# A pool for gathered expert rows, clears and square roots on ScalarE, and three shared parts behind the expert blocks, in an eight-stage adaLN network

## The chip, the cores and the metric

The kernel runs on one core of a Trainium2 chip, as one program and one launch. The metric is the device time of one execution in microseconds (us); the time of a kernel is the median of several executions. The core has a matrix engine (TensorE, PE in the profile), a vector engine (VectorE, DVE), an engine for activations (ScalarE, ACT), a general engine (GpSimd, POOL) and a queue processor (SyncE, SP). Each works through its own list of instructions in order; they wait for one another by semaphores. ScalarE looks functions such as Exp, Ln and Gelu up in a table that has to be loaded first, by an instruction of its own.

## The reference, cut to what matters

The network has four layers on 32 sequences of 256 tokens with 128 features. Each layer has two halves of the same form, with shift, scale and gate from a condition vector of each sequence:

```
for L in range(4):
    h = layernorm(x) * (1 + ca) + sa;  x = x + ga * attn_L(h)
    h = layernorm(x) * (1 + cb) + sb;  x = x + gb * ffn_L(h)
```

`layernorm` divides by sqrt(var + 1e-5). The eight halves differ:

- stage 0, a two-branch selective scan; stage 2, local softmax attention mixed with chunked linear attention on several Haar levels; stage 4, attention with a learned phase; stage 6, attention over a latent of 32 features;
- stage 1, a mixture of 8 experts, top 2 of a softmax, with a shared expert beside them:

```
shared = gelu(h @ Wfc_s + bfc_s) @ Wproj_s + bproj_s
routed = sum over the two chosen e of gate[e] * (gelu(h @ Wfc[e] + bfc[e]) @ Wproj[e] + bproj[e])
```

- stage 3, a mixture of 8 experts with a capacity of 512 rows: router `relu(h @ rw1 + rb1) @ rw2 + rb2`, top 2, positions counted by a running sum, rows beyond the capacity dropped;
- stage 5, a mixture over parts of the features; stage 7, a gated MLP with its operands rounded to blocks of 4-bit numbers.

## The kernel before, in words

The activations `x` stay in SBUF, as 16 blocks (`NB`) of 512 tokens with the features on the 128 partitions. A stage is a function (`dense_moe`, `hale`, `capacity_moe`, and so on) that works block by block. Inside a stage the order of the work is written by hand: `put(t, f, ...)` hangs a piece of work on slot `t` of an agenda, and the slots are then emitted in rising order. Four slots make one round, in which block `b` starts its norm while older blocks are in later steps. With `strict` on, TensorE's instructions keep program order, and those of VectorE inside `kept()`; `strict_act` does the same for ScalarE. Everything else is placed by a scheduler, which may move an instruction ahead of others on its engine if nothing it depends on forbids it. Tiles come from pools; when a pool is closed its memory goes to later pools, and a write to it has to wait for the last use of what lay there.

Norms have three forms. `norm_stats` and `norm_apply` transpose a block into PSUM, take mean and variance on VectorE, find the inverse root, and scale. The inverse root is `rsqrt` (Ln and Exp on ScalarE, one Newton step of four operations on VectorE) or, where `newton` is set, `rsqrt_newton` (an integer first guess and four Newton steps, 14 small operations on VectorE, L998 to L1005). `norm_rows` with `norm_apart` is stage 6's form: `norm_roots` is Ln and Exp on ScalarE (`ln_t`, `ln_rs`), the Newton step and the scaling are on POOL. `use_ln_exp` (L410) loads the table that holds both Ln and Exp, in program order.

**Stages 1 and 2.** Stage 1 routes 16 blocks (logits, top 2, positions, and 8 indirect DMAs by POOL that scatter a block's rows into `regions`), then `route_totals` works out which rows form the 39 expert blocks (`idx_...`), then POOL fetches weights (`wts`) and rows (`dk`) for one expert block after another. `shared_part(m, a, i)` is the shared expert of a block, in four parts: parts 0 and 1 are the hidden layer with Gelu on ScalarE, parts 2 and 3 the output, and at the end the residual into `x`. Before, block `b` has them at slots `4b + 24` to `4b + 27`; routing ends at slot 72, and the shared parts of blocks 12 to 15 lie between it and the first expert block. The expert outputs `eo` go to DRAM (`expert_rows`). In stage 2, `gather_rows` brings a block's two expert rows of each token back by indirect DMA into `got`, `gather_sum` weights and adds them into `gy`, and `gather_end` adds them to `x`. Stage 2 begins with clearing on POOL (L1630, L1632, L1639): `mts` and `vzb`, `vzl` (zero, with ones in columns 8 to 16 of each head) and `kvs`.

**Stages 3 and 4** have the same form: a router (`router_hidden`, `router_sums`, `router_choice`, `capacity_slots`, with `disp` as the target of the scatter), eight experts, and the gather in stage 4. `attention_pools` clears `mts` and `vzs` on POOL (L1338). Stages 4 and 6 both call it.

**Stage 6** runs a block's attention heads on TensorE (`S`, `po`), with Exp on ScalarE (`E`, L1471), while the norm, projections and the front of stage 7's MLP (`fx`, `xT`) of neighbouring blocks are slotted between them.

Of the kernel before, what the change touches and what calls it, by code (L numbers as in the profile page):

```python
# [20 lines left out]
F = mybir.dt.float32  # L21
# [4 lines left out]
ALU = mybir.AluOpType  # L26
# [296 lines left out]
class Program:  # L323
# [129 lines left out]
    def norm_rows(self, src, small=None, tag="ln_xn"):  # L453

        nc = self.nc
        ps = self.ps("tp", (P, 4, P))
        for t in range(4):
            self.tr(ps[:, t, :], src[:, t * P : (t + 1) * P])
        xn = self.wk(tag, (P, 4, P))
        self.act(xn, ps, AF.Copy)  # L460
        st, mv, v = self.wk("ln_st", (P, 4, 6)), self.wk("ln_mv", (P, 4, 2)), self.wk("ln_v", (P, 4))
        for t in range(4):
            nc.vector.bn_stats(st[:, t, :], xn[:, t, :])
        for t in range(4):
            nc.vector.bn_aggr(mv[:, t, :], st[:, t, :])
        (small or nc.vector).tensor_scalar(v, mv[:, :, 1], 1e-5, None, ALU.add)
        return xn, mv, v

    def norm_place(self, xn, mv, v):
# [539 lines left out]
    def dense_moe(self, w):  # L1009
# [8 lines left out]
        with ExitStack() as ctx:  # L1018
# [19 lines left out]
            def put(t, f, *args):  # L1038
                agenda.setdefault(t, []).append((f, args))

            for b in range(NB):
                a = {"b": b}
                T = 4 * b
                put(T + 1, lambda a: a.update(xn=self.norm_apply(*a["st"])), a)
                put(T + 0, lambda a: a.update(st=self.norm_stats(self.x[a["b"]])), a)
                put(T + 3, lambda a: a.update(h=self.norm_out(a["xn"], self.ada_mods(0, 1, a["b"]), "h")), a)
                put(T + 5, self.route_logits, m, a)
                put(T + 10, self.route_slots, m, a)
                put(T + 13, self.route_gates, m, a)
                for i in range(4):  # L1050
                    put(T + 24 + i, self.shared_part, m, a, i)
            end = 4 * NB + 8
# [223 lines left out]
    def block_out(self, m, a, t):  # L1276
# [11 lines left out]
        if t == 3:  # L1288
# [3 lines left out]
            self.nc.sync.dma_start(m["eo"][j * n : (j + 1) * n, :].rearrange("(t p) f -> p t f", p=P), eo)  # L1292

    def gather_rows(self, b, t):


        got = self.gather[b, t] = self.wk("got", (P, 2, P))
        for k in (0, 1):
# [9 lines left out]
    def gather_sum(self, b, t):  # L1308

        nc, got = self.nc, self.gather.pop((b, t))  # L1310
        if t == 0:
            self.gather["y", b] = self.wk("gy", (P, 4, P))
        y = self.gather["y", b]
# [16 lines left out]
    def attention_pools(self, ctx):  # L1330

        self.pools(ctx, {"S": 3, "po": 1, "tp": 1}, E=5, ln_xn=1, vp=1, oc=2, got=4)
        self.far = ctx.enter_context(self.tc.tile_pool(name="far", bufs=2, space=DRAM))
        keep = ctx.enter_context(self.tc.tile_pool(name="zeros", bufs=1))
        self.mts = [keep.tile([P, 2, P], F, name=f"mt{n}") for n in range(4)]
        self.vzs = [keep.tile([P, 16, 32], F, name=f"vz{n}") for n in range(8)]
        for t in self.mts + self.vzs:
            self.nc.gpsimd.memset(t, 0.0)  # L1338

# [276 lines left out]
    def hale(self, w):  # L1616
        nc, c = self.nc, self.c
        BF = mybir.dt.bfloat16
        with ExitStack() as ctx:
            once = "hm wl sw mx identb loc0b loc1b kt kvs lv dT gv gs y mT sg_a av al".split()  # L1620
            self.pools(ctx, {"S": 2, "po": 1, "tp": 3}, E=6, h=3, got=4, gy=1, **dict.fromkeys(once, 1))
            ps, wk = self.ps, self.wk
# [5 lines left out]
            self.vzl = [keep.tile([P, 4, 16, 32], F, name=f"vzl{t}") for t in (0, 1)]  # L1628
            for t in self.mts + self.vzb + self.vzl:
                nc.gpsimd.memset(t, 0.0)  # L1630
            for t in self.vzb + self.vzl:
                nc.gpsimd.memset(t[:, :, :, 8:16], 1.0)  # L1632
            self.identb = wk("identb", (P, P), BF)
# [4 lines left out]
            self.kvs = wk("kvs", (P, 5, SEQ))  # L1638
            nc.gpsimd.memset(self.kvs, 0.0)  # L1639
            self.kt = wk("kt", (P, 5, P))  # L1640
# [19 lines left out]
            self.gather = None  # L1660

    def hale_slots(self, w):

# [6 lines left out]

        tiles = {}
        for q in range(2 * NB):
            b, s = divmod(q, 2)
# [402 lines left out]
    def capacity_moe(self, w):  # L2076
# [3 lines left out]
        with ExitStack() as ctx:  # L2080
# [6 lines left out]
            self.pools(ctx, {"tp": 2, "hid": 3, "o": 1, "s": 2}, zero=1, ht=4, dk=4, hid=3, eo=3, h=3)  # L2087
            self.strict = self.newton = True
            zero = self.wk("zero", (P, 8 * P))
# [14 lines left out]
            for b in range(NB):  # L2104
                a = {"b": b}
                T = 4 * b
                put(T + 1, lambda a: a.update(xn=self.norm_apply(*a["st"])), a)
                put(T + 0, lambda a: a.update(st=self.norm_stats(self.x[a["b"]])), a)
# [15 lines left out]
            for t in sorted(agenda):  # L2124
                for f, args in agenda[t]:
                    f(*args)
            self.strict = self.newton = False
            self.gather = {"eo": eo, "rows": 8 * CAP}
# [681 lines left out]
    def run(self):  # L2810
# [10 lines left out]
        self.begin()  # L2821
        names = [f"s{n}" for n in self.stages]
        for n, name in enumerate(names):
            self.load(name)
            if n + 1 < len(names):
                self.load(names[n + 1])
            bodies[int(name[1:])](self.weights.get(name))
        if self.stages[-1] != 7:
            with ExitStack() as ctx:
                self.pools(ctx, {"tp": 4})  # L2830
                for b in range(NB):
                    if self.gather:
# [3 lines left out]
                        self.gather_end(self.stages[-1] // 2, b)  # L2836
                    self.store(b, self.out.rearrange("(b t p) f -> b p t f", p=P, t=4))


# [32 lines left out]
```

## Time and profile before

| | |
|---|---|
| median of 13 executions | 6515.45 us (6508.58 to 6534.99) |
| profiled execution, its own time | 6527.31 us |
| its span | 6525.5 us |
| mean granted TensorE clock | 0.937 |
| PE, DVE, ACT, POOL busy | 88%, 64%, 53%, 44% of the span |
| ACT table loads, 1283 ns each | 44 |
| stage 1, routing | about 1040 to 1300 us |
| stage 1, first expert block on TensorE | 1329.26 us |
| stage 2, first gather | 1648.31 us |
| stage 3, routing | 3704 to 3945 us |
| stage 4, first gather | 4042.55 us |
| stage 6 | 5517 to 6265 us, a block every 44.7 us |

The times in the trace are microseconds from the start of the span. In a line of the timeline the first number is the start, the second the duration, then come the engine, the line of the program, the operation and `output<-inputs` with their shapes; `x4` says how many instructions the line sums up. In brackets stands how long the engine stood idle before, and whose work ended that wait. L310, L399, L403 and L406 are lines of helpers (VectorE in program order, matmul, transpose, activation), so the tile's name tells which step it is. "remote" is a wait whose releaser the profile doesn't show. The clock of TensorE varies; where it is 0.5 a matmul takes twice as long.

### The profile page before, as it was taken

The page shows a single profiled execution, that of the slowest core. Times are in us where ns is not written, and L with a number is a line of the kernel's source. Part 1 is how long each engine was busy: PE and PEld are TensorE (multiplying, and loading weights), DVE is VectorE, ACT ScalarE, POOL GpSimd, SP SyncE. Part 2 cuts the span into 40 slices and gives each one's busy share as a digit, 9 for nine tenths or more (in the row PEclk, how much of TensorE's full clock was granted, in tenths as well). Part 3 has the DMA queues.
Part 4 walks back from the last instruction along what each step waited for, and adds up shares of the span by engine and source line. Part 5 has one row for each costly group of instructions (what it writes and reads, how often), then busy time and mean ns, then how long its engine had stood idle before and what let it go on. Part 6 is the DMA issues. An engine that isn't in the chain of part 4 may idle for free. (4 is left out here: it accounts for less than half of the span.)

```text
span 6525.5 us, 132602 instructions
## 1 busy us (share of the span) xinstructions
PE 5765.2 (88%) x54369; PEld 3286.2 (50%) x54369; DVE 4206.9 (64%) x9329; ACT 3473.0 (53%) x5045; POOL 2857.3 (44%) x3202
## 2 busy tenths in 40 slices
PE   6888886999899999999999776999979998999987
PEld 4666664467455555555555433455522222455544
DVE  4777776611466666666665562888767774677678
ACT  5888884333344444454444331444458887555532
POOL 4565563565444544444444352444334545222200
PEclk7899997999899999999999877999989999999988
DMA  2110111145000000000000101111034443000010
GB/s 63 42 43 31 41 42 37 44 120 127 16 6 5 7 6 5 6 7 5 6 3 2 48 1 36 23 29 29 25 81 90 92 90 75 14 20 20 19 35 29
DMA packets 175875, 232.17 MB, mean 36 GB/s; under 512 B 46567, under 2 KB 95967, under 8 KB 175010
## 3 DMA queue, kind: packets, MB, share of 16 engines
q1 hardware_dynamic: 124880, 126.50, 7.6%
q0 software_dynamic: 26992, 56.62, 3.7%
q10 hardware_dynamic: 23394, 40.58, 1.7%
q8 instruction: 427, 7.00, 0.5%
q14 instruction: 182, 1.49, 0.1%
HBM read 88.21 MB, written 74.97 MB: 25 GB/s over the span
## 5 line engine op out<-in xcount | busy, mean ns | idle before, releaser
L310 DVE TENSOR_REDUCE mt<-S 128x4 f32<-128x1024 f32 (+2 forms) x768 | 755.7, 999 | 538.3 <-PE S L399 534.8
L910 DVE TENSOR_TENSOR_SCAN hs<-decay,dB 128x512 f32<-128x512 f32 x512 | 583.3, 1205 | 159.0 <-PE dB L399 118.1
L1471 ACT ACTIVATE E<-S 128x1024 f32<-128x1024 f32 x448 | 457.8, 1022 | 427.6 <-PE S L399 385.3
L406 ACT ACTIVATE hid<-S,bigw 128x1024 f32<-128x1024 f32 x512 | 537.2, 1111 | 124.7 <-PE S L399 124.2
L1962 POOL TENSOR_SCALAR_AFFINE_SELECT E<-E 128x1024 f32<-128x1024 f32 x320 | 348.7, 1092 | 580.9 <-ACT E L1961 580.5
L310 DVE TENSOR_TENSOR E<-S,cst 128x1024 f32<-128x1024 f32 x320 | 391.2, 1223 | 286.7 <-PE S L399 285.8
L399 PE MATMUL S<-qa,kx 32*128 32x256 f32 x4096 | 511.4, 372 | 11.9 <-DVE mt L310 11.3
L399 PE MATMUL S<-kx,q 32*128 32x512 f32 (+1 forms) x2048 | 513.8, 595 | 3.0 <-POOL kx L1607 2.7
L2509 POOL TENSOR_TENSOR acc<-acc,ye 128x512 f32<-128x512 f32 x256 | 344.4, 1345 | 361.3 <-DVE ye L310 318.2
L1961 ACT COPY E<-S 128x1024 f32<-128x1024 f32 x320 | 323.5, 1011 | 324.6 <-PE S L399 312.7
L399 PE MATMUL S<-qG,f 32*128 32x512 f32 x2560 | 366.8, 643 | 47.5 <-DVE E L310 47.5
L399 PEld LDWEIGHTS S<-qa,kx 32*128 32x128 f32 x4096 | 326.1, 185 | 96.5 <-DVE mt L310 64.2
L403 PE MATMUL hT<-cst,hs 128*128 128x128 f32 x2048 | 300.5, 293 | 68.7 <-ACT hsT L406 64.6
L399 PE MATMUL S<-hm,bigw 32*128 32x512 f32 x2048 | 339.0, 654 | 24.7 <-ACT hid L406 24.7
L406 ACT ACTIVATE decay<-dl,A 128x510 f32<-128x510 f32 x512 | 338.5, 712 | 0.0
L406 ACT ACTIVATE hsT<-hT 128x1024 f32<-128x1024 f32 x256 | 259.8, 1015 | 124.8 <-PE hT L403 124.3
L399 PE MATMUL po<-hid,bigw 128*32 128x512 f32 x2048 | 277.7, 615 | 30.6 <-DVE ye L310 30.6
L403 PEld LDWEIGHTS hT<-cst,hs 128*128 128x128 f32 x2048 | 236.7, 149 | 121.6 <-ACT hsT L406 103.9
L1837 ACT ACTIVATE E<-S 128x768 f32<-128x768 f32 (+1 forms) x192 | 169.0, 880 | 237.7 <-PE S L399 237.6
L310 DVE TENSOR_TENSOR ye<-po,gb 128x512 f32<-128x512 f32 x256 | 176.1, 688 | 176.0 <-PE po L399 103.2
L399 PE MATMUL po<-E,vz 128*32 128x256 f32 x4096 | 287.5, 365 | 0.3 <-ACT oc L1491 0.2
L399 PE MATMUL po<-E,vzl 128*32 128x128 f32 x8192 | 276.8, 276 | 0.0
(540 smaller groups left out, 13005.8 us busy)
## 6 DMA issues: line engine op xcount, KB each, us to landing
gb<-gT SPq DMA_DIRECT2D x256, 256.0 KB
regions<-zeros ACTq DMA_DIRECT2D x16, 2048.0 KB
rx<-far SPq DMA_DIRECT2D x64, 256.0 KB
expert_rows<-eo SPq DMA_DIRECT2D x39, 256.0 KB
xin<-in_x SPq DMA_DIRECT2D x16, 256.0 KB
out<-out SPq DMA_DIRECT2D x16, 256.0 KB
xTd<-xT SPq DMA_DIRECT2D x15, 256.0 KB
xT<-xTd SPq DMA_DIRECT2D x15, 256.0 KB
```

What stands on the lines that cost most here:

```text
L310: return lambda *args, **kw: self.tc.keep_in_program_order(op(*args, **kw))
L399: return self.tc.keep_in_program_order(self.nc.tensor.matmul(out, lhsT, rhs, start=start, stop=stop, **kw))
L403: return self.tc.keep_in_program_order(self.nc.tensor.transpose(out, in_, self.c.ident[:k, :k]))
L406: ins = self.nc.scalar.activation(*args, **kw)
L910: nc.vector.tensor_tensor_scan(hs[:, :, n], decay, dB[:, :, n], 0.0, ALU.mult, ALU.add)
L1471: nc.scalar.activation(e, src, AF.Exp, scale=scale)
L1837: nc.scalar.activation(e, src, AF.Exp, scale=1.0 / math.sqrt(8))
L1961: nc.scalar.copy(e, src)
L1962: nc.gpsimd.affine_select(e, e, [[0, 8], [1, P]], ALU.is_ge, 0.0, base=0, channel_multiplier=-1)
L2509: nc.gpsimd.tensor_tensor(a["acc"], a["acc"], ye, ALU.add)
```

## The change

1. The tiles of the gathered rows, `got` (4 buffers) and `gy` (1 buffer), come from a pool of their own, `rows_pool`, which is opened ahead of stages 1 and 3 and closed behind stages 2 and 4. Before, they were in the pools of stages 2 and 4.
2. `clear` writes zeros by copies on ScalarE, in pieces of at most 512 columns, from a tile of zeros. It takes the place of POOL's memsets in `attention_pools` and in stage 2; there it hangs on a slot, as `hale_zeros`.
3. Stage 3's norm uses `norm_turned`: `rsqrt` in place of `rsqrt_newton`, and the scaling by four passes of ScalarE from PSUM in place of four of VectorE. The table for Ln and Exp is loaded when the stage begins.
4. The shared parts of blocks 9, 10 and 11 of stage 1 move from slots 60 to 71 to slots 252 to 263, behind the last expert block.

```diff
--- before.py
+++ after.py
@@ -466,6 +466,17 @@
+    def norm_turned(self, ps, mv, v):
+
+        nc = self.nc
+        rs, shift = self.wk("ln_rs", (P, 4)), self.wk("ln_m", (P, 4))
+        self.rsqrt(rs, v, "ln")
+        nc.vector.scalar_tensor_tensor(shift, mv[:, :, 0], -1.0, rs, ALU.mult, ALU.mult)
+        xn = self.wk("ln_xn", (P, 4, P))
+        for n in range(4):
+            self.act(xn[:, n, :], ps[:, n, :], AF.Identity, bias=shift[:, n : n + 1], scale=rs[:, n : n + 1])
+        return xn
+
     def norm_place(self, xn, mv, v):
 
         rs = self.wk("ln_rs", (P, 4))
@@ -1047,8 +1058,11 @@
                 put(T + 5, self.route_logits, m, a)
                 put(T + 10, self.route_slots, m, a)
                 put(T + 13, self.route_gates, m, a)
+
+
+                last = 4 * (8 + blocks + b + 7) if 9 <= b < 12 else T + 24
                 for i in range(4):
-                    put(T + 24 + i, self.shared_part, m, a, i)
+                    put(last + i, self.shared_part, m, a, i)
             end = 4 * NB + 8
             put(end, self.route_totals, m)
             for j in range(blocks):
@@ -1291,10 +1305,24 @@
             j, n = a["j"], m["BLK"]
             self.nc.sync.dma_start(m["eo"][j * n : (j + 1) * n, :].rearrange("(t p) f -> p t f", p=P), eo)
 
+    def rows_tile(self, tag, shape, bufs):
+
+        return self.rows_pool.tile(list(shape), F, name=tag, tag=tag, bufs=bufs)
+
+    def clear(self, tiles):
+
+        for t in tiles:
+            n = len(t.shape)
+            flat = t.rearrange({2: "p a -> p a", 3: "p a b -> p (a b)", 4: "p a b c -> p (a b c)"}[n])
+            size = flat.shape[1]
+            for at in range(0, size, 4 * P):
+                part = flat[:, at : min(at + 4 * P, size)]
+                self.nc.scalar.copy(part, self.zeros[:, : part.shape[1]])
+
     def gather_rows(self, b, t):
 
 
-        got = self.gather[b, t] = self.wk("got", (P, 2, P))
+        got = self.gather[b, t] = self.rows_tile("got", (P, 2, P), 4)
         for k in (0, 1):
             self.nc.gpsimd.indirect_dma_start(
                 out=got[:, k, :],
@@ -1309,7 +1337,7 @@
 
         nc, got = self.nc, self.gather.pop((b, t))
         if t == 0:
-            self.gather["y", b] = self.wk("gy", (P, 4, P))
+            self.gather["y", b] = self.rows_tile("gy", (P, 4, P), 1)
         y = self.gather["y", b]
         at = slice(4 * b + t, 4 * b + t + 1)
         with nc.vector.kept():
@@ -1329,13 +1357,12 @@
 
     def attention_pools(self, ctx):
 
-        self.pools(ctx, {"S": 3, "po": 1, "tp": 1}, E=5, ln_xn=1, vp=1, oc=2, got=4)
+        self.pools(ctx, {"S": 3, "po": 1, "tp": 1}, E=5, ln_xn=1, vp=1, oc=2)
         self.far = ctx.enter_context(self.tc.tile_pool(name="far", bufs=2, space=DRAM))
         keep = ctx.enter_context(self.tc.tile_pool(name="zeros", bufs=1))
         self.mts = [keep.tile([P, 2, P], F, name=f"mt{n}") for n in range(4)]
         self.vzs = [keep.tile([P, 16, 32], F, name=f"vz{n}") for n in range(8)]
-        for t in self.mts + self.vzs:
-            self.nc.gpsimd.memset(t, 0.0)
+        self.clear(self.mts + self.vzs)
 
     def slot(self, vz, head):
 
@@ -1618,7 +1645,7 @@
         BF = mybir.dt.bfloat16
         with ExitStack() as ctx:
             once = "hm wl sw mx identb loc0b loc1b kt kvs lv dT gv gs y mT sg_a av al".split()
-            self.pools(ctx, {"S": 2, "po": 1, "tp": 3}, E=6, h=3, got=4, gy=1, **dict.fromkeys(once, 1))
+            self.pools(ctx, {"S": 2, "po": 1, "tp": 3}, E=6, h=3, **dict.fromkeys(once, 1))
             ps, wk = self.ps, self.wk
             keep = ctx.enter_context(self.tc.tile_pool(name="zeros", bufs=1))
             self.mts = [keep.tile([P, 2, P], F, name=f"mt{n}") for n in range(4)]
@@ -1626,17 +1653,12 @@
 
             self.vzb = [keep.tile([P, 2, 16, 32], F, name=f"vzb{t}") for t in (0, 1)]
             self.vzl = [keep.tile([P, 4, 16, 32], F, name=f"vzl{t}") for t in (0, 1)]
-            for t in self.mts + self.vzb + self.vzl:
-                nc.gpsimd.memset(t, 0.0)
-            for t in self.vzb + self.vzl:
-                nc.gpsimd.memset(t[:, :, :, 8:16], 1.0)
             self.identb = wk("identb", (P, P), BF)
             self.locb = wk("loc0b", (P, P), BF), wk("loc1b", (P, 192), BF)
             nc.vector.tensor_copy(self.identb, c.ident)
             nc.vector.tensor_copy(self.locb[0], c.locq0)
             nc.vector.tensor_copy(self.locb[1], c.locq1)
             self.kvs = wk("kvs", (P, 5, SEQ))
-            nc.gpsimd.memset(self.kvs, 0.0)
             self.kt = wk("kt", (P, 5, P))
 
             self.wl = wk("wl", (P, 4, 2, P))
@@ -1659,6 +1681,13 @@
             self.strict = False
             self.gather = None
 
+    def hale_zeros(self):
+        self.clear(self.mts + self.vzb + self.vzl + [self.kvs])
+        ones = self.c.ones.rearrange("p (h e) -> p h e", e=8)
+        for t in self.vzb + self.vzl:
+            n = t.shape[1]
+            self.nc.scalar.copy(t[:, :, :, 8:16], ones.unsqueeze(1).to_broadcast([P, n, 16, 8]))
+
     def hale_slots(self, w):
 
 
@@ -1669,6 +1698,7 @@
             agenda.setdefault(t, []).append(work)
 
         tiles = {}
+        put(side, -47, self.hale_zeros)
         for q in range(2 * NB):
             b, s = divmod(q, 2)
             a = {"b": b, "s": s, "mt": self.mts[2 * s : 2 * s + 2]}
@@ -2085,7 +2115,8 @@
             disp = self.keep_dram.tile([8 * CAP, P], F, name="disp")
             eo = self.keep_dram.tile([8 * CAP, P], F, name="eo")
             self.pools(ctx, {"tp": 2, "hid": 3, "o": 1, "s": 2}, zero=1, ht=4, dk=4, hid=3, eo=3, h=3)
-            self.strict = self.newton = True
+            self.strict = True
+            self.use_ln_exp()
             zero = self.wk("zero", (P, 8 * P))
             nc.gpsimd.memset(zero, 0.0)
             for z in range(4):
@@ -2104,7 +2135,7 @@
             for b in range(NB):
                 a = {"b": b}
                 T = 4 * b
-                put(T + 1, lambda a: a.update(xn=self.norm_apply(*a["st"])), a)
+                put(T + 1, lambda a: a.update(xn=self.norm_turned(*a["st"])), a)
                 put(T + 0, lambda a: a.update(st=self.norm_stats(self.x[a["b"]])), a)
                 put(T + 3, lambda a: a.update(h=self.norm_out(a["xn"], self.ada_mods(1, 1, a["b"]), "h")), a)
                 put(T + 5, self.router_hidden, m, a, 0)
@@ -2124,7 +2155,7 @@
             for t in sorted(agenda):
                 for f, args in agenda[t]:
                     f(*args)
-            self.strict = self.newton = False
+            self.strict = False
             self.gather = {"eo": eo, "rows": 8 * CAP}
 
     def router_hidden(self, m, a, i):
@@ -2820,11 +2851,18 @@
         ]
         self.begin()
         names = [f"s{n}" for n in self.stages]
+        rows = None
         for n, name in enumerate(names):
             self.load(name)
             if n + 1 < len(names):
                 self.load(names[n + 1])
+            if name in ("s1", "s3"):
+                rows = ExitStack()
+                self.rows_pool = rows.enter_context(self.tc.tile_pool(name="rows", bufs=1))
             bodies[int(name[1:])](self.weights.get(name))
+            if rows and name in ("s2", "s4"):
+                rows.close()
+                rows = None
         if self.stages[-1] != 7:
             with ExitStack() as ctx:
                 self.pools(ctx, {"tp": 4})
@@ -2835,6 +2873,8 @@
                             self.gather_sum(b, t)
                         self.gather_end(self.stages[-1] // 2, b)
                     self.store(b, self.out.rearrange("(b t p) f -> b p t f", p=P, t=4))
+        if rows:
+            rows.close()
 
 
 def prepare(inputs):
```

## The prediction

> **What bounds the kernel now.** I read the page's engine shares first, then the table of busy time by stretch, to see which stages TensorE fills, then the timeline around each edited place, and last the order of the changed kernel's instructions on each engine.
>
> ```profile
> PE 5765.2 (88%) x54369; PEld 3286.2 (50%) x54369; DVE 4206.9 (64%) x9329; ACT 3473.0 (53%) x5045; POOL 2857.3 (44%) x3202
> ...
> PE   6888886999899999999999776999979998999987
> ```
>
> TensorE is the bound: 88% of the span, and 9 tenths in most slices. The slices at 6 and 7 are the scan, the two routings and the boundaries, and the edits aim there. But one edit reaches stage 6 (5517 to 6265), where a block takes 44.7 us and the stretch 5740 to 5785 has PE busy for 44.01 of 45 us: there no ScalarE delay is free if TensorE waits for it.
>
> **Stage 6: the activation table, +32.** This is the largest term, and the diff does not show it. `attention_pools` now clears on ScalarE with copies that wait for nothing. The scheduler moves stage 6's twelve copies, and its load of the Ln/Exp table with them, up into the tail of stage 2. In between, stages 4 and 5 load other tables. In the changed order ScalarE therefore has a load before each Ln and another before each Exp in stage 6: 31 norms (16 in attention, 15 in the front of the MLP), 62 loads; before, one load at 5515 served all. A load's price is in stage 5, where they stand already:
>
> ```profile
> 5023.56 1.28 ACT L406 ACT_TABLE_LOAD   x1
> 5024.86 0.63 ACT L406 ACTIVATE ex<-ex 128x512 f32<-128x512 f32 x1
> 5025.51 1.28 ACT L406 ACT_TABLE_LOAD   x1
> ```
>
> The next instruction starts 0.02 us after each load, so 62 x 1.28 = 79.5 us of ScalarE. How much reaches TensorE? The first norm of a block, and then the second:
>
> ```profile
> 5716.86 0.21 ACT L406 ACTIVATE ln_t<-ln_v 128x4 f32<-128x4 f32 x1 [2.87 <-POOL ln_v L466]
> ...
> 5717.10 0.21 ACT L406 ACTIVATE ln_rs<-ln_t 128x4 f32<-128x4 f32 x1
> 5717.21 1.00 ACT L1471 ACTIVATE E<-S 128x1024 f32<-128x1024 f32 x1
> ...
> 5718.11 0.59 ACT L406 ACTIVATE xT<-tp 128x512 f32<-128x512 f32 x1
> ...
> 5718.75 1.98 PE L399 MATMUL tp<-oT,w 128*128 128x512 f32 x4
> ```
>
> ```profile
> 5730.46 0.20 ACT L406 ACTIVATE ln_rs<-ln_t 128x4 f32<-128x4 f32 x1
> 5730.57 1.00 ACT L1471 ACTIVATE E<-S 128x1024 f32<-128x1024 f32 x1
> ...
> 5732.10 0.64 PE L399 MATMUL po<-E,vz 128*32 128x256 f32 x8
> ```
>
> The load ahead of Ln is free: it runs in the 2.87 us (second norm: 1.53) in which ScalarE waits for `ln_v`. The load ahead of Exp is not. In the first norm E and `xT` queue behind it; `tp<-oT` starts 0.05 us after `xT` ends, because it needs that PSUM tile, so TensorE stands 1.28 us. In the second, E would end at 5732.85 instead of 5731.57, and `po<-E` starts at 5732.10: 0.8 us late. Steady blocks: 14 x 1.28 + 14 x 0.8 = 29; the first and last norms, where little overlaps, another 3 x 1.28, makes 33; 1 us off for the 0.4 us waits on VectorE's `mt` that can absorb some. I take +32. Bounds: 0 (all hidden) and 79.5 (all exposed); I stand nearer the row that shows `xT` without slack. POOL's chain after Exp also starts 1.3 us later, but its scaled `ln_xn` is done at 5721.67 and transposed only at 5725.33.
>
> The Trainium skill bears on this edit: "ScalarE: Activation LUTs", section "Table sets: the hidden batching unit", says to group activations by table set, and the section "What ACT_TABLE_LOAD costs" puts a switch at 1283 ns of load plus about 1380 ns of drain. The rows above agree with the first figure and show no drain; by the page's 2.66 us the exposed half alone would be some 70 to 80 us instead of 32.
>
> **Rows pool, stage 3 to 4: -5.** POOL's memsets stand ahead of the first gather, since both wait for memory that the last `eo` store reads:
>
> ```profile
> 4037.33 1.13 POOL L1338 MEMSET mt<- 128x256 f32 x4 [91.22 <-DMA eo<-eo]
> ...
> 4042.55 1.05 POOL L1299 DMA_INDIRECT got<-eo,back  x1 [0.16 <-issue]
> ```
>
> With the memsets gone the gathers issue from about 4037.3: 5.2 us earlier, and the sums on VectorE, the residual and the norm that follow are one chain. ScalarE's 12 copies (4 of 0.38, 8 of 0.58, by its copies of that size) and a table load end by 4046; its next work that matters, `ln_xn`, was at 4057.43 and moves to 4052. Covered.
>
> **Stage 1 to 2: gathers free, but three shared parts in front: +10.**
>
> ```profile
> 1635.84 0.69 DVE L1290 COPY eo<-o 128x512 f32<-128x512 f32 x1 [4.11 <-PE o L399]
> ...
> 1638.96 1.32 POOL L1630 MEMSET mt<- 128x256 f32 x4 [21.41 <-DMA expert_rows<-eo]
> ...
> 1648.31 1.01 POOL L1299 DMA_INDIRECT got<-expert_rows,back  x1 [0.16 <-issue]
> ```
>
> The gathers could come 9.35 us earlier. But a shared part is 18 TensorE passes; b=13's took 1291.86 to 1300.0, so 8.4 us, and three are 25 us: TensorE from 1635.8 to 1661, with 12 Gelus of 0.69 on ScalarE inside that; they issue no DMA and pass no queue of SP or POOL. VectorE's order has their residuals ahead of the casts, `sw`, `wl` and the gather sums. So: residual done 1662.1, casts 0.85, `mx` and `sw` to 1664.2, `wl` and the second `sw` to 1667.2, eight sums of 0.33 to 1669.8, residual, transposes and statistics 3.7 (1660.45 to 1664.17 before): 1673.5. ScalarE, after `sw` at 1664.4, has a load (1.28), 14 clears (13 x 0.49 pitch + 0.38) and four copies of ones (about 1.9): 1674.4, then `ln_t`, which was at 1664.17. So +10, ends +5 and +14.
>
> **Stage 1's routing: -14.** The same 25 us leave slots 60 to 71. In the rounds there, 13.6 us apart against 12.97 in rounds without a shared part, that is 3 x 0.7 = 2. More at the end: between `s<-both` of b=14 (1271.07) and of b=15 (1280.93) TensorE does nothing but shared parts, about 8 of the 9.9 us. Shared parts of b=12 to 15 (4 x 8.4) follow, and only then the first expert block:
>
> ```profile
> 1317.84 0.69 ACT L406 ACTIVATE hid<-hid,w 128x512 f32<-128x512 f32 x1 [13.54 <-remote]
> ...
> 1329.26 0.60 PE L403 MATMUL tp<-cst,dk 128*128 128x128 f32 x4
> ```
>
> Ten us earlier, TensorE would reach this block near 1319 with the stall, near 1306 without it. The stall (ScalarE 13.5, VectorE 13.2) overlaps the burst of weight gathers (1301 to 1308), whose cause the trace does not show, so it may stay, shrink or fall elsewhere. The expert's rows are there by about 1306 (POOL's issues, minus 5). So -6 to -23; I take -14, nearer to the end where the stall stays.
>
> **Stage 3's roots: -16 over the rounds, +4 at the start.** A round there is 13.8 us and runs through VectorE:
>
> ```profile
> 3840.64 0.95 PE L403 MATMUL tp<-cst,x 128*128 128x128 f32 x4
> ...
> 3846.43 1.36 DVE L448 TENSOR_SCALAR ln_xn<-tp,ln_mv,ln_rs 128x128 f32<-128x128 f32 x4
> ...
> 3848.08 0.19 DVE L1090 TENSOR_TENSOR both<-rt_o,rt_o 128x32 f32<-128x32 f32 x1
> ```
>
> VectorE loses 14 small operations and the 1.36, and gets 5 small ones. From `tp<-x` as zero: statistics end at 2.5, Ln behind the first `hid` copy at 2.7, Exp behind the second at 3.8, the five operations (interleaved with the choice's, 0.11 apart) at 4.95, then four ScalarE passes. The nearest row is `h`, 128x256 from PSUM with both pointers, 0.56 long and 0.46 apart; at 128 columns 0.36 apart, so 1.5: 6.57, against 7.15 now. `both` comes at about 6.65 instead of 7.63. I take 1.1 of a round, 14.5 rounds: -16. Ends: -28 (two us a round) and +5, if ScalarE's in-order copies (`hid`, `lT`, `ht`) hold the passes up. At the start ScalarE is busy issuing loads until 3702.95 while VectorE norms ahead; now the first root waits for that: 0.4 + 1.0 + 1.5 + a transpose 0.9 = +4.
>
> **Stage 2's tail: +2.** The hoisted copies and the load fall between `dT` (3672.77) and `gs` (3676.80), where ScalarE's gaps are 1.34, 0.49 and 0.49: the load (1.28) and two copies (1.16) do not fit, about 2 late.
>
> **Sum.** 32 - 5 + 10 - 14 - 16 + 4 + 2 = +13. The profiled execution took 6527.31 (span 6525.5), 12 above the median of 6515.45: 6540 by its own clock, 6528.5 against the median. About 0.2%, 13 us, is what a measurement of this kernel can tell from no change, so the forecast lies on that line.
>
> **Rivals.**
> - *The exposed loads are hidden* (stage 6 at 0 to 10). For: ScalarE is busy for only about 25 of 45 us there. Against: `tp<-oT` waits for `xT` with no slack. 6497 to 6507, faster from a stage 6 cost under 6. Chance 0.15.
> - *The stall in stage 1 vanishes and the rounds of stage 3 gain two us each*: -23 and -28 in place of -14 and -16, 6507. Against: the burst is still there, and can stall both engines elsewhere. Chance 0.12.
> - *The loads cost more than one per norm*, both on the path in part: +55 in stage 6, 6552. Chance 0.15.
> - *Moving the shared parts only moves them*: the tail of stage 1 keeps its stall and gains 6, the boundary loses 14: 6540. Chance 0.15.
> - *The sum as above*: 0.43, within 10 us of 6528.5, a little more than half of it beyond the line.
>
> So faster 0.2, same 0.25, slower 0.55. From the rivals' ends, 6500 to 6565.
>
> **What would show it.** In the changed profile: about 63 more table loads, stage 6 blocks of near 46.8 us in place of 44.7, `tp<-oT` waiting for `xT`; first gathers right behind the last store in stages 2 and 4; the first expert block of stage 1 near 1315; stage 3 rounds near 12.7. Blocks still at 44.7 in stage 6 would make the prediction wrong on the faster side; a first `ln_t` of stage 2 less than 5 us after its old distance from the last `eo` would also.

## The result, and the profile after

The changed kernel took 6559.12 us (median of 10 executions, 6546.28 to 6571.4) against 6518.8 us (median of 44) before: a ratio of 1.0063 [1.0053, 1.0073], or +40 us. Its profiled execution took 6562.62 us (span 6560.8, mean granted clock 0.941), 35.3 us more than the profiled execution before. The forecast was +13 with the slower side as the likeliest. The direction holds, the amount does not: 27 us of the cost were not in the sum.

The page after, engine shares and the row of PE by slices:

```profile
PE 5751.9 (88%) x54369; PEld 3280.4 (50%) x54369; DVE 4170.5 (64%) x9121; ACT 3598.4 (55%) x5251; POOL 2846.2 (43%) x3165
...
PE   6888886899899999999999766999889998999976
```

VectorE lost 208 instructions and ScalarE's busy time rose from 53% to 55%, while TensorE's work is the same, 54369 matmuls. A total does not say where 35 us went. The same event in both traces does (us from the start of the span):

| event | before | after | offset |
|---|---|---|---|
| stage 1, first `dT` of the expert blocks | 1330.26 | 1327.57 | -2.7 |
| stage 1, last `eo` | 1635.84 | 1636.61 | +0.8 |
| stage 2, `ln_t` of the first block | 1664.17 | 1674.39 | +10.2 |
| stage 2, `h` of the second block | 1714.02 | 1715.19 | +1.2 |
| stage 2, `h` of the last block | 3446.55 | 3460.99 | +14.4 |
| stage 3, `h` of the first block | 3702.99 | 3722.06 | +19.1 |
| stage 3, first scatter | 3722.60 | 3740.54 | +17.9 |
| stage 3, last scatter | 3945.14 | 3963.94 | +18.8 |
| stage 3, last `eo` | 4033.76 | 4052.01 | +18.3 |
| stage 4, first gather | 4042.55 | 4055.93 | +13.4 |
| stage 6, `h` of the first block | 5533.10 | 5542.07 | +9.0 |
| stage 6, `h` of the last block | 6175.34 | 6212.40 | +37.1 |

**Stage 6: +28.1** between its first and last `h`. The groups of ScalarE in the changed kernel have the loads (line, engine, operation, count, then busy time and mean ns of one):

```profile
L406 ACT ACT_TABLE_LOAD x98 | 125.7, 1283 | 2.8 <-PE g L399 1.1
```

It was x37 before: 61 more at this line, 107 in all against 44. One block of stage 6 in the timeline of the changed kernel:

```profile
5774.37 1.28 ACT L406 ACT_TABLE_LOAD   x1
...
5777.23 0.21 ACT L406 ACTIVATE ln_t<-ln_v 128x4 f32<-128x4 f32 x1 [1.57 <-POOL ln_v L466]
...
5777.45 1.28 ACT L406 ACT_TABLE_LOAD   x1
...
5778.74 0.21 ACT L406 ACTIVATE ln_rs<-ln_t 128x4 f32<-128x4 f32 x1
5778.86 1.01 ACT L1498 ACTIVATE E<-S 128x1024 f32<-128x1024 f32 x1
...
5779.76 0.59 ACT L406 ACTIVATE xT<-tp 128x512 f32<-128x512 f32 x1
...
5780.40 3.36 PE L399 MATMUL tp<-oT,w 128*128 128x512 f32 x4 [1.31 <-ACT xT L406]
```

The first load stands in ScalarE's wait for `ln_v`, which shrank from 2.87 us to 1.57: it is free. The second stands between Ln and Exp, and TensorE's idle time before `tp<-oT` is 1.31 us, with `xT` named as the cause.

**Stage 3 to 4: -4.9** from the last `eo` to the first gather (8.79 before, 3.92 now). The timeline after has the gather ahead of any clearing on POOL, and the clearing on ScalarE beside it:

```profile
4052.01 0.69 DVE L2247 COPY eo<-o 128x512 f32<-128x512 f32 x1 [6.17 <-PE o L399]
...
4055.49 1.33 ACT L1320 COPY mt<-zeros 128x256 f32<-128x256 f32 x4 [8.80 <-DMA eo<-eo]
4055.93 1.05 POOL L1327 DMA_INDIRECT got<-eo,back  x1 [91.02 <-DMA eo<-eo]
```

**Stage 1 to 2: +9.45, then given back.** The three shared parts stand behind the last expert block, and the first `ln_t` comes 37.78 us after the last `eo` instead of 28.33:

```profile
1636.61 0.69 DVE L1304 COPY eo<-o 128x512 f32<-128x512 f32 x1 [4.12 <-PE o L399]
...
1660.95 0.88 DVE L570 SCALAR_TENSOR_TENSOR x<-o,mods,x 128x256 f32<-128x256 f32 x2 [7.24 <-PE o L399]
...
1674.39 0.21 ACT L406 ACTIVATE ln_t<-ln_v 128x4 f32<-128x4 f32 x1
```

At the second block's `h` the offset is +1.2 only. The table of busy time by stretch says why. One row each, the kernel before and then after; the columns are the length, the busy time of PE, PEld, DVE, ACT and POOL with the instructions in brackets, the granted clock, the DMA share and GB/s:

```profile
1680.00:1690.00 10.00, 10.00 (x28) 3.85 (x25) 4.70 (x7) 0.00 (x0) 1.95 (x2) 0.50 0.05 13
```

```profile
1680.00:1690.00 10.00, 8.59 (x43) 4.21 (x44) 4.86 (x9) 2.03 (x3) 2.21 (x3) 0.93 0.08 19
```

TensorE was busy for the whole stretch before and got 28 matmuls through at half clock. After, it got 43 through in less time. In that trace of before the half clock lasted from 1643 to 1691, in the trace of after from 1668 to 1681.

**Stage 1's routing: -2.7, not -14.** The timeline after:

```profile
1316.22 0.60 PE L403 MATMUL tp<-cst,dk 128*128 128x128 f32 x4
...
1322.68 0.88 DVE L570 SCALAR_TENSOR_TENSOR x<-o,mods,x 128x256 f32<-128x256 f32 x2 [13.50 <-remote]
...
1327.57 0.69 DVE L1281 COPY dT<-tp 128x512 f32<-128x512 f32 x1 [4.01 <-remote]
...
1328.31 5.30 PE L399 MATMUL hid<-dT,wts 128*128 128x512 f32 x6 [11.49 <-issue]
```

TensorE transposes the first expert's rows at 1316.22, 13.0 us earlier than before. But a stall of 13.5 us has moved with the work: it now holds VectorE, and the copy `dT`, without which TensorE has nothing to do, waits until 1327.57.

**Stage 3's rounds: +0.9, not -16.** The waits of the changed kernel, summed by waiting tile and releaser (total us, count, longest):

```profile
DVE ln_st L435 <- remote: 46.5, 4, 13.2
...
ACT hid L406 <- remote: 27.3, 5, 7.1
ACT ht L406 <- remote: 22.6, 4, 6.3
```

Before, there were three such waits in stage 3, 11.0, 6.7 and 5.0 us long. The rounds no longer take 13 to 15 us each. From scatter to scatter they go 10.24, 20.79, 13.20, 10.24, 20.71, 12.10 and so on: a round bound by POOL's eight scatters, then a long one. The timeline of a long one:

```profile
3836.89 1.06 PE L403 MATMUL tp<-cst,x 128*128 128x128 f32 x4
...
3847.44 0.97 POOL L1148 DMA_INDIRECT disp<-ht,si  x1 [0.30 <-issue]
3849.47 0.89 DVE L435 BATCH_NORM_STATS2 ln_st<-tp 128x6 f32<-128x128 f32 x4 [12.55 <-remote]
...
3850.88 0.69 ACT L406 ACTIVATE hid<-hid,bigw 128x512 f32<-128x512 f32 x1 [6.43 <-remote]
...
3859.20 0.97 POOL L1148 DMA_INDIRECT disp<-ht,si  x1 [10.79 <-ACT lT L406]
```

POOL issues 16 scatters back to back here, up to 3848.41. Under the second eight VectorE stands for 12.55 us with a releaser that the profile doesn't show, until 3849.47, and afterwards POOL in turn for 10.79. What VectorE's statistics read, the transposes `tp<-cst,x`, had ended by TensorE's own record at 3837.95, 11.5 us before they start.

**Stage 2's body: +13.3, in no step of the prediction.** Between the `h` of the second and of the last block the offset grows in four steps of about 3.3 us and stays flat in between. One step, two stretches of the changed kernel (columns as above):

```profile
1850.00:1856.00 6.00, 4.42 (x66) 2.44 (x68) 3.39 (x6) 4.25 (x8) 2.19 (x2) 0.96 0.01 3
1856.00:1862.00 6.00, 6.00 (x26) 3.40 (x22) 3.00 (x7) 2.29 (x5) 1.09 (x1) 0.50 0.00 0
```

In the second stretch TensorE gets 26 matmuls through at clock 0.50; before, 89 at clock 1.00, behind an equal first stretch.

### The profile page after: what moved, and what is told of

The parts are those of the page before. It is cut to its first block, busy times and chain, and to the rows that moved or that the text cites. A ratio compares the mean times of both kernels' runs of the same rounds, so it can differ in the third digit from the quotient of the medians.

```text
span 6560.8 us, 132520 instructions
## 1 busy us (share of the span) xinstructions
PE 5751.9 (88%) x54369; PEld 3280.4 (50%) x54369; DVE 4170.5 (64%) x9121; ACT 3598.4 (55%) x5251; POOL 2846.2 (43%) x3165
```

## The experiments

They ran in three groups, each on its own chip, with the kernel before beside them: on chip A the kernel before took 6458.77 us, on B 6528.37, on C 6449.72. The median time and the ratio are against that. "Rounds" is the time from the first scatter of stage 3 to the last, 16 blocks of eight.

**Stage 6's clearing back to POOL** (chip A), the rest as in the changed kernel:

```diff
 def attention_pools(self, ctx):
...
-        self.clear(self.mts + self.vzs)
+        if self.by_pool:                  # set in stage 6
+            for t in self.mts + self.vzs:
+                self.nc.gpsimd.memset(t, 0.0)
+        else:
+            self.clear(self.mts + self.vzs)
```

> The changed kernel, with stage 6's clears by POOL's memsets again; ScalarE then has 45 table loads in place of 107. Theory (the loads ahead of Exp stand on TensorE's path in stage 6): stage 6 goes back to about 44.7 us a block and the time falls by 28, to about 6531 (6525 to 6537). Rival (the loads are hidden, stage 6 lost its 28 us to something else, such as the clock or the place of the clears): within 8 us of the changed kernel, 6551 to 6567.

6437.24 us, ratio 0.9970 [0.9957, 0.9982]. Table loads fall to 45, and stage 6 is 643.7 us long from first to last `h` (642.2 before, 670.3 in the changed kernel). The wait for `xT` in stage 6 is gone: one of 0.7 us is left, against 15.9 us over 12. It is not a wait of the memsets that keeps the load in stage 6: on POOL, too, they run in the tail of stage 2, from 3650.6 us in this trace and from 3667.9 in the kernel before, while the load stands at 5427.1 and 5515.2. Only copies on ScalarE take the load along.

**Stage 6's clearing alone on ScalarE** (chip A), in the kernel before:

```diff
-        for t in self.mts + self.vzs:
-            self.nc.gpsimd.memset(t, 0.0)
+        if self.by_act:                   # set in stage 6
+            self.clear(self.mts + self.vzs)
+        else:
...
```

> The kernel before, with one edit: stage 6's clears by ScalarE, so that the load of the Ln/Exp table moves up and 62 loads come in stage 6. Theory: stage 6 alone costs 28, and the hoisted copies about 2 in the tail of stage 2: 6547 (6541 to 6556). Rival (loads hidden): within 8 us of the kernel before, 6511 to 6527.

6487.15 us, 1.0043 [1.0029, 1.0057], which is +28.4. Loads rise to 106, stage 6 to 667.1 us. So this edit alone costs what stage 6 lost in the changed kernel. The waits that carry it:

```profile
PE tp L399 <- ACT xT L406: 16.6, 13, 1.6
```

```profile
PE tp L400 <- ACT xT L407: 16.3, 13, 1.3
```

The first is the changed kernel, the second this run: 13 waits each, 16.6 and 16.3 us; one of them, of 0.7, is in the kernel before too. That is the part put at 14 x 1.28 = 17.9. The part put at 14 x 0.8 = 11.2 is there as well, but not at `po<-E`, where the prediction had it. In the changed kernel:

```profile
PE tp L403 <- ACT lat L2579: 9.6, 13, 0.7
```

`lat` is the copy that stands behind E on ScalarE; TensorE's next transposes need its PSUM tile. In this run the waits for it are 9.5 us over 13, in the kernel before and in the run above there are none, and no TensorE wait for E before `po` is among the waits of stage 6 in the changed kernel.

**Stage 3's old roots** (chip A), in the changed kernel:

```diff
-            self.strict = True
-            self.use_ln_exp()
+            self.strict = self.newton = True
...
-   put(T + 1, lambda a: a.update(xn=self.norm_turned(*a["st"])), a)
+   put(T + 1, lambda a: a.update(xn=self.norm_apply(*a["st"])), a)
```

> The changed kernel, with stage 3's norm as before (14 operations of VectorE for the root, scaling by VectorE). Theory (the rounds with two blocks' scatters back to back are followed by stalls of 10 us that eat the shorter chain, and the start costs 4): 3 to 5 faster than the changed kernel, 6555, rounds of about 13.8 without long stalls. Rival (the shorter chain gains 16 and the stalls in the profiled run are an accident of that run): 12 slower, 6571.

6494.33 us, 1.0058 [1.0044, 1.0071], with executions from 6482.49 to 6501.36. The rounds take 183.94 us here; in the first run of this group, which has the new roots, 162.30. So on this chip the new roots gain 21.6 us, more than the 16 of the forecast, and lose 3 at the start (first `h` 22.7 us after stage 2's last residual instead of 19.2). By the medians the gain is larger still: 6494.33 is 28.7 above the first run of this group with the 28.4 of stage 6 added to it. So the rival had the direction here. The two traces of the result show nothing of it.

**Shared parts at their old slots** (chip A), in the changed kernel:

```diff
-                last = 4 * (8 + blocks + b + 7) if 9 <= b < 12 else T + 24
+                last = T + 24
```

> The changed kernel, with the shared parts of blocks 9 to 11 at their old slots. Theory (moving them gains nothing in stage 1, costs 9.5 at the boundary, and TensorE's clock gives 9 back by the second block of stage 2): within 6 of the changed kernel, 6553 to 6565; the first Ln of stage 2 then comes 5 to 9 earlier, and the clock is 0.5 again until about the second block's start. Rival (the boundary's 9.5 are a loss that stays): 8 to 10 faster, 6550.

6456.46 us, 0.9997 [0.9988, 1.0006]. Here `ln_t` comes 20.63 us after the last `eo`: the pool of rows gains 7.7 at this place, and the moved parts cost 17.2 (37.78 less 20.63). What they gain: the first `dT` is at 1312.97 and 1307.47 in the two runs of this chip with the old slots, at 1298.89 and 1295.97 in the two with the new ones. So the move gains 9 to 17 there, of which 6.5 are gone by the last `eo` (314.7 us behind the first `dT` instead of 308.2), and then loses 17. From the medians, the first run of this group less this one, with the 28.4 of stage 6 put back, the move costs 9 us. That is the rival: the boundary's loss stays, and the clock doesn't give it back. The second block's `h` is at 1683.84 here, at 1693.37 and 1690.53 in the two runs with the new slots.

**The changed kernel again** (chip B), no edit:

> The changed kernel itself, beside the kernel before. In the traces of the undone edits stage 3 lost no time to waits without a shown releaser; in the two traces of the changed kernel and the kernel before it did (46.5 us of them for the changed one's statistics on VectorE). Theory (the loss in stage 3 belongs to the conditions of a run, not to the kernel): where those waits are missing, stage 3's rounds are 10.2 us, and the changed kernel is only 8 to 12 slower than the kernel before, ratio 1.0012 to 1.002. Rival (the changed kernel always pays them): ratio 1.006 again, with the waits in its trace.

6567.94 us, 1.0060 [1.0045, 1.0075]. The result repeats, with the stalls, as the rival said:

```profile
DVE ln_st L435 <- remote: 33.6, 3, 14.0
```

**The kernel before again** (chip B), no edit:

> The kernel before, for a trace under the same conditions as the others of this set. Theory: stage 3's rounds of 11.8 instead of 13.8 and no gaps of a microsecond between VectorE's dependent operations, where the conditions are those of the undone edits; 13.8 with the gaps where they are those of the first traces.

6517.42 us, one execution. Its rounds take 213.54 us, most of them 13.2 to 15.1 each, and in stage 3 no wait has an unshown releaser. The changed kernel on this chip has 226.69. So where the stalls fall, the new roots cost 13 us over the rounds instead of gaining. (The profiled execution before had 222.54, with 22.7 us of stalls in it; that is why the two profiles of the result differ there by 0.9 only.)

**No loads in stage 6, no moved parts** (chip B): `by_pool` and `last = T + 24` as above; the pool of rows, the other clears and the new roots stay.

> The changed kernel, with stage 6's clears by POOL and the shared parts of blocks 9 to 11 at their old slots. Theory (the loads cost 28, the moved shared parts 7 to 9 at the boundary): 25 to 30 faster than the kernel before where stage 3 has no waits without a releaser, ratio 0.9955 to 0.996; some 5 faster where it has. Rival (the moved parts cost nothing): the same as with the clears alone undone, ratio 0.997.

6529.97 us, 1.0002 [0.9992, 1.0012]. The 7.6 us at stage 2's start and the 4.9 at stage 4's are there (20.66 and 3.93 in place of 28.26 and 8.78), and stage 3 eats them: rounds 226.89, in the same pattern of 10.25, 21.04, 13.28, with these waits in stage 3:

```profile
DVE ln_st L436 <- remote: 50.5, 4, 14.0
ACT hid L407 <- remote: 29.0, 6, 7.2
```

From 6529.97 to 6567.94 are 38 us for the loads and the moved parts; less 28.4, the move costs 9.6 here, as it did on chip A.

**Stage 3's new roots alone** (chip B), in the kernel before: `norm_turned` and `use_ln_exp` as in the change, nothing else.

> The kernel before, with stage 3's roots and scaling by ScalarE as the only edit. Theory (a shorter chain down to what POOL's scatters take, 10.2 a round; the start about 3 later): 25 to 30 faster than the kernel before without those waits, within 5 with them. Rival (the 16 of the prediction): 12 faster.

6537.72 us, 1.0013 [1.0001, 1.0025], +9. Rounds 227.54, 14 more than the kernel before on this chip, waits of `ln_st` on an unshown releaser 48.3 us over 4. Neither the pool, the clears nor the moved parts are in this kernel, so the new roots alone bring as much of these waits as the whole change does. They are not the only way to them: the profiled execution before has 22.7 us of them in stage 3 without the new roots.

**Pauses behind each block's scatters** (chip C), in the kernel of the run without loads and moved parts. The theory was that VectorE's stalls follow 16 scatters without a gap, so POOL gets idle work behind each eight (three memsets, or one):

```diff
-        self.scatter(m, a, si, 8 * CAP)
+        with nc.gpsimd.kept():
+            self.scatter(m, a, si, 8 * CAP)
+            for _ in range(3):            # 1 in the second kernel
+                nc.gpsimd.memset(m["zero"], 0.0)
```

> The changed kernel with neither stage 6's loads nor the moved shared parts, and with three more POOL memsets of 128x1024 (about 2.9 us, on a tile that is zero already) behind each block's scatters in stage 3: work added, so that two blocks' scatters no longer stand back to back. Theory (uninterrupted scatters of two blocks on POOL make VectorE and ScalarE wait 10 us and more, without a shown releaser): where those waits occur, they go, all rounds are 13.1 to 13.5, and stage 3 is 15 to 25 shorter than without the memsets, 6505 to 6515 on conditions in which the kernel before takes 6528. Where they don't occur, rounds go from 10.2 to 13.1 and the kernel is 45 longer. Rival (the waits have nothing to do with POOL's issues): the rounds are longer by 2.9 each in either case, 35 to 45 slower.

> The same with one memset (0.95 us). Theory: a gap of 1.2 us in place of 0.3 is hardly enough: some of the long waits remain, between the kernel without memsets and the one with three. Rival (no part in it): 15 slower than without memsets.

6466.61 us, 1.0028 [1.0018, 1.0037], and 6440.77 us, 0.9984 [0.9975, 0.9993]. On this chip no stall fell in any kernel, so neither run could take one away. What they do show is the bound. POOL in the timeline with three memsets:

```profile
3810.03 0.97 POOL L310 DMA_INDIRECT disp<-ht,si  x1 [0.30 <-issue]
3810.99 3.00 POOL L310 MEMSET zero<- 128x1024 f32 x3
...
3814.15 0.97 POOL L310 DMA_INDIRECT disp<-ht,si  x1 [0.16 <-DVE ln_mv L438]
```

Rounds are 13.07 us with three, 11.04 with one, 10.21 with none (the last run of this group): POOL's eight scatters and what stands between them set the round, to the tenth. Whether a gap would end the stalls on chip B was not tried.

**Pool of rows and the clears of stages 2 and 4 alone** (chip C): stage 6 on POOL, old slots, old roots.

> Of the change only the rows pool and the clears of stages 2 and 4 by ScalarE; stage 6's clears by POOL, stage 3's roots by VectorE, shared parts at their old slots. Theory (gathers 9.35 and 5.2 earlier, of which ScalarE's clears and TensorE's clock take a part): 6 to 14 faster than the kernel before, ratio 0.998 to 0.999. Rival (the gathers' start is covered by something else): same within 3.

6440.46 us, 0.9985 [0.9976, 0.9994], -9.3. The two boundaries gain 7.8 and 4.9 in the trace, 12.7 together; 9.3 of it is in the time.

**The first experiment again** (chip C), no edit to it:

> The changed kernel with stage 6's clears by POOL once more, beside the others of this set. Theory (loads 28, moved shared parts about 10, stage 3 between +9 and -28 by the conditions): ratio 1.0015 to 1.002 where stage 3 has the waits, 0.997 where it has not. Rival (ratio 0.997 is what the kernel gives everywhere): 0.997 with the waits too.

6443.14 us, 0.9987 [0.9978, 0.9996]. The gain over before is -6.6, on chip A it was -21.5. Of these 15 us, 9 are the kernel before, which is that much faster on C. The intervals meet between 0.9978 and 0.9982. The rounds are 162.37 as on chip A, so it lies elsewhere; where is not settled.

## Why the prediction was right and where it was not

**Right: the direction, and stage 6.** The largest term was read from the changed order of instructions, not from the diff: copies that wait for nothing rise into stage 2 and take a table load along. +32 was predicted; 28.1 and 27.5 were measured from first to last `h` in the changed kernel's two traces, and 28.4 in the time of the run that has this edit alone (24.9 from first to last `h` there). The split was right too, half free ahead of Ln, half exposed, the first norms through `xT` (17.9 in the sum, 16.6 measured). For the second norms the size was right (11.2 in the sum, 9.6 measured) and the place was not: the load delays `lat`, and `po<-E` reads an E that is done earlier. In the changed kernel `po` starts 0.25 us after the delayed E does, at 5795.39, and waits for nothing. The Trainium skill's "ScalarE: Activation LUTs", section "What ACT_TABLE_LOAD costs", states a drain of about 1380 ns besides the load, and the estimate from it was 70 to 80; no row here shows that drain, since the next ACTIVATE starts 0.01 us after a load that ended at 5778.73.

**Luck: the place in the range.** 6559.12 lies inside 6500 to 6565, six us from its end, and no rival describes how it came there: the nearest, 6552, has the loads at +55, and they cost 28. Terms of the sum were off by more than the margin that was left.

**Right: the pool, the tail, the start.** Stage 3 to 4 -5 (-4.87), the boundary to stage 2 +10 (+9.45), the tail of stage 2 +2 (+1.7, `dT` to `gs`), the start of stage 3 +4 (+3.6).

**Wrong by 29: "I take 1.1 of a round, 14.5 rounds: -16".** The step took a round as a chain through VectorE whose links have fixed lengths, and shortened it. The chain did shorten: on chips A and C rounds of mostly 11.5 to 12.5 became 10.21, and 20 to 22 us were gained. On chip B rounds of 13 to 15 became a repeated 10.2, 12.8 and 21, and 13 us were lost. The +5 end of the range stood for another mechanism, ScalarE's copies in the way. The row that could have warned was shown in the prediction's own part on stage 1, a stall of 13.5 us under a burst of POOL's indirect DMAs "whose cause the trace does not show". Once the norm is shorter, POOL issues 16 scatters without a break in stage 3 too. The prediction carried the stall in one stage and not in the other. The runs with single edits say how much of the gap this is, though they ran on different chips. The roots with their start cost 9.3 (chip B) where -12 stood; the moved parts cost 9 to 10 (A and B) and the pool with its clears gains 9.3 (C), together about 0 where -9 stood; the loads cost 28.4 (A) where 34 stood with stage 2's tail. That is +38 of the +40 measured: of the 27 that were missing the roots are 21, stage 1 and the boundaries 9, and the loads give 6 back.

**Partly wrong: stage 1, -14.** "It may stay, shrink or fall elsewhere" was right in words; the value was not the end where it stays. It fell on VectorE's `x` and `dT`: -2.7 in the profiled execution. On chip B the first `dT` came 8.8 us earlier (1330.43 against 1339.26), on A 9 to 17. Against the 17.2 that the moved parts cost at the boundary, the move loses 9 to 10 us on both chips. The rival that the move only moves was right in kind: it had 8 for it. (A shared part is 8.1 us in the row that the prediction reads, 1291.86 to 1299.98, not 8.4; that moves its 25 us by 1.)

**Unforeseen, in the profiles alone: the clock.** In the two profiles, 9 us were given back at stage 2's start and 13 lost in its body. Neither is a fixed price of the edits. The first block of stage 2 to the second took 46.6 us in the kernel before and 46.4 in the run with the new roots alone, and 37.4 to 38.9 in eleven others, with and without every edit (44.7 in one); the kernel before itself has 38.9 in its other trace. With the moved parts the first stretch of half clock at that boundary is 13.7 us long in all five traces, with the old slots 20 to 48 us in nine; whether the move keeps the long ones away was not tried. Between second and last block, the traces read 1732.5, 1735.8, 1738.7, 1742.4 or 1745.8 us, some 3.3 apart: the granted clock has no, one, two, three or four dips to 0.50 of 6.8 us in that stretch. The kernel before has none in one trace and two in the other, the changed kernel four and three. Old and new slots both have 1732.5 and 1739.0 among them. Here they come to 13.3 less 9, so the two profiles' 35.3 lies near the medians' 40 in part by luck: the rounds' 12 us are missing in it.

"TensorE: Matmul & The Clock Gate", Part 1, says that the clock falls to half after a window of about 3.4 us of idling, and that the window runs freely. The free running fits that the dips come and go; the idling does not, as the stretch ahead of the dip has PE busy for 4.42 of 6 us, and an equal 4.43 before was followed by no dip.

**What the stalls wait for.** A releaser that the profile's views don't name can still be found in the trace's own list of semaphore updates. In the two traces of the result every wait of more than 2.5 us on an unshown releaser, in stages 1 and 3 alike, is for a semaphore that only TensorE's instructions update, and the update comes long after TensorE's record of the work has ended: at 3849.44 in the round shown, 11.5 us behind `tp<-cst,x`. In the first experiment's trace on chip A no such update comes more than 0.25 us behind. TensorE's ends are modelled, so this alone doesn't tell a late matmul from a late signal.

VectorE's ends are recorded, and its signals are late too: in stage 3 of the kernel before, an addition ends at 3849.63, its update comes at 3850.16, and the next one, which needs it, starts at 3850.19; on chip A the three times are 3845.81, 3845.82 and 3845.84. Between the first scatter of stage 3 and the last, the changed kernel has 659 instructions of VectorE that update its semaphore; the trace of the result holds 456 such updates in that time, those of chip B 455 to 458, those of chips A and C 656 to 659. The kernel before is no exception (516 and 520 of 815 in its two traces). So late signals come with the conditions of a run, not with the change. But the kernel with the shorter norm loses more to them: its rounds in stage 3 take 64 us more on chip B than on A (226.69 against 162.30), with the old norm 30 us more (213.54 against 183.94).

**Open.** Why the signals are late in stages 1 and 3, where POOL issues its indirect DMAs, and why chips A and C have next to none. That the scatters are the reason is argued from the place alone. No version beat the first experiment clearly; the pool and the new roots without the loads and the moved parts were run on chip B alone without pauses (1.0002).

## What to carry to other kernels

An operation that waits for nothing is free to move, and on a new engine it can take along what is tied to that engine. Before a memset goes to another engine, look where the scheduler puts it and which table load travels with it: 62 loads cost 28 us in a stage that the edit was not aimed at. Work moved off one boundary onto another is priced at both, and an unexplained stall that a trace shows under a kind of traffic belongs in the price of every edit that makes such traffic denser.

## What the runs showed that was not expected

- Under POOL's indirect DMAs in stages 1 and 3, VectorE and ScalarE stood up to 22.6 and 19.1 us (stage 1 of the run without loads and moved parts) without a releaser in the profile. All six traces of the result and of chip B have such stalls (that of the kernel before on B in stage 1 alone), and none of the eight of the two other chips.
- Where the stalls fall, small dependent operations of VectorE come apart as well. Below are two of the three additions of the running sum in a round of stage 3, from the timeline of the kernel before, and then all three from the first experiment's timeline on chip A:

```profile
3850.19 0.17 DVE L1096 TENSOR_TENSOR past<-past,both 128x8 f32<-128x8 f32 x1 [0.48 <-DVE rt_p L624]
3850.91 0.17 DVE L1096 TENSOR_TENSOR past<-past,both 128x8 f32<-128x8 f32 x1 [0.56 <-DVE past L1096]
```

```profile
3845.64 0.57 DVE L1111 TENSOR_TENSOR past<-past,both 128x8 f32<-128x8 f32 x3
```

  Gaps of half a microsecond in the one, none in the other. The kernel before is itself 70 us slower on chip B than on A (6528.37 against 6458.77). Beside the run on A that differs from it in stage 6 alone, its first `dT` of stage 1 comes 32 us later, and stage 3's rounds take 30 us more: these two routings are most of it.
- The half clock at stage 2's start lasted 48 us in one trace of the kernel before and 31 in another (until 1691 and 1681), and stage 2's body lost 3.3 us at a time to dips, none to four of them in a trace.
